# Building the matrices with C on their diagonals by DMA instead of by VectorE, in the state space scans of a four-layer network

## The chip, the core and the metric

The kernel runs on one core of a Trainium2 chip. Its engines are TensorE (PE, with its weight loads as PEld), VectorE (DVE), ScalarE (ACT), GpSimd (POOL) and SyncE (SP), which here issues nearly all transfers. Sixteen DMA engines move the data between DRAM and SBUF. The metric is the device time of one execution in microseconds (us). The time before the change is the median of 3 runs.

## The reference, cut to what matters

The reference applies four layers in turn, each as `x = x + layer(groupnorm(x))`, to an image batch of 4 x 96 x 56 x 56 in float32: softmax attention (layer 0), a selective scan in eight directions (layer 1), attention over the best eight of a local window (layer 2), and a scan in four directions with a bottleneck (layer 3). The change touches layer 1 alone. Its core, for each image, each of 8 directions, 192 channels and 16 states, over L = 3136 time steps:

```python
xs = cross_scan(xc)                      # rows, columns, diagonals, antidiagonals, and each backwards
x_dbl = einsum('bkdl,kcd->bkcl', xs, x_proj_weight)
dts, Bmat, Cmat = split(x_dbl, [R, R + N], axis=2)          # R = 6, N = 16
delta = softplus(einsum('bkrl,kdr->bkdl', dts, dt_projs_weight) + dt_projs_bias)
def step(hc, inp):
    u_t, d_t, B_t, C_t = inp
    hc = hc * exp(d_t[..., None] * A) + (d_t * u_t)[..., None] * B_t[:, :, None, :]
    return hc, einsum('bkdn,bkn->bkd', hc, C_t)
```

The last line is what the changed matrices serve: at each time step the 16 states of a channel are multiplied by that step's 16 values of C and added up.

## The kernel before

The layers follow one another. Layer 1 first projects, convolves and writes the four orders of the image to DRAM (`into_scan`), then runs `scans`, then gathers the eight directions and normalises. `scans` is the part that is changed, and all of it stands in one order written out by hand: within `in_order`, every engine executes its instructions exactly in the order in which the program issues them.

Two images lie together on the 128 partitions (64 channels each), the 192 channels are three blocks `j`, and the 3136 steps are seven chunks of 448. Two pairs, eight directions and seven chunks make 112 chunks. The 16 states are four groups `g` of four. A piece is (chunk, `j`, `g`), so a chunk has 12 pieces and the main loop (L712) turns 12 times for a chunk. In a turn:

- `inputs` (L614, POOL) makes `q` = delta times u times B for the piece two turns ahead, from `du` and the tile `bm` that holds B of the group, broadcast over partitions.
- `factor` (L622, ACT) makes `e` = exp(delta A), one state at a time, into three PSUM buffers, so up to three states ahead.
- `scan` (L634, DVE) runs four recurrences of 448 steps, in place in `q`; `carry` (L640, ACT) keeps the last state for the next chunk.
- `turned` (L650, PE) transposes the previous piece's `q`, `kept` (L659, ACT) copies it out of PSUM as `ht`, and `outputs` (L671, PE) multiplies it by `cd` and adds it to `y`. Time step t is m x 14 + c; after the transpose a partition is (state, m), with 4 states and 32 values of m. `cd` therefore holds, for every image half, group and c, a 128 x 32 matrix with four 32 x 32 diagonals, one for each state, and C on them. The matmul picks each step's own C and sums over the states.
- `gather` (L684, L685, DVE; L693, SP) copies a finished `y` and stores it after the third block.

Beside the twelve turns, the generator `prepare` makes what the next chunk needs. The main loop calls it once at the end of each of the turns 0 to 7, and `fetch` in turns 8 to 11:

- turn 0: load `u` (L551, SP); turn 2: project it (L557, PE), copy to `xd` (L561, ACT), store the rows of B and C to the DRAM tile `bc` (L564, SP, two DMAs)
- turn 3: load C from `bc` as `cv`, 128 partitions (state, m) of 112 values (L570, SP, two DMAs in pieces of 14 values)
- turn 5: project delta (L578, PE) and apply softplus (L580, ACT, with a change of the activation table before and after it), then VectorE multiplies `cv` by a repeated 32 x 32 identity (`same`) into `cd` (L585): 3584 values per partition, all but one in 32 of them zero
- turn 6: `du` = delta times u (L594, POOL)
- turns 8 to 11: `fetch` loads the four `bm` tiles (L604, SP, two DMAs each)

SP issues these in program order, and waits at an instruction until its operands have landed and its buffer is free. It runs ahead of the other engines where nothing holds it. There are six `bm` buffers, so SP can load the first two of the next chunk before the current chunk releases one. `out` is stored at turn 1, ahead of `bc`.

Of the kernel before, what the change touches and what calls it, by code (L numbers as in the profile page):

```python
# [9 lines left out]
F32 = mybir.dt.float32  # L10
AF = mybir.ActivationFunctionType
ALU = mybir.AluOpType
# [6 lines left out]
CH = 448  # L19
NCH = L // CH  # L20
# [25 lines left out]
def spread(ap, n):  # L46

    p, c = ap.shape
    return ap.unsqueeze(1).to_broadcast([p, n, c])
# [20 lines left out]
class Net:  # L70
# [435 lines left out]
    def scans(self, us, dram, ks):  # L506
# [3 lines left out]
        nc, tc = self.nc, self.tc  # L510
        ng = 4
        ngrp = NS // ng
        nk = len(ks)
        NT = 32
        NC = CH // NT
# [4 lines left out]
        with in_order(tc), ExitStack() as cx:  # L520
            wp = cx.enter_context(tc.tile_pool(name="sw", bufs=1))
            st1 = cx.enter_context(tc.tile_pool(name="sst", bufs=2))
            bp = cx.enter_context(tc.tile_pool(name="sbig", bufs=6))
# [3 lines left out]
            pst = cx.enter_context(tc.tile_pool(name="spt", bufs=2, space=PSUM))  # L527
            psy = cx.enter_context(tc.tile_pool(name="spy", bufs=1, space=PSUM))
            xpw, dtw, dtb, al = (self.load(wp, f"l1_{n}") for n in ("xpw", "dtw", "dtb", "alog"))
            same = self.load(wp, "k_same")  # L530
            na = wp.tile([128, nk, NB, NS], F32, name="na")
            nc.scalar.activation(na, al, AF.Exp)
            nc.vector.tensor_scalar(na, na, -1.0, None, ALU.mult)
# [1 line left out]
            def wide():  # L535
                return pst.tile([128, 2, 512], F32, name="t")

            chunks = []
            for pr in range(NPAIR):
                for k, (o, rev) in enumerate(ks):  # L540
                    for i in range(NCH):
                        chunks.append(dict(
                            pr=pr, k=k, src=us[pr][o], rev=rev, i=i, c=NCH - 1 - i if rev else i,
                        ))
            states = {}

            def prepare(s):

                k, c = s["k"], s["c"]
                u = p2.tile([128, NB, CH], F32, name="u", bufs=3)  # L550
                nc.sync.dma_start(u, s["src"][:, :, c * CH : (c + 1) * CH])  # L551
                s["u"] = u
                yield
                yield
                p = wide()[:, 0]
                for j in range(NB):
                    nc.tensor.matmul(  # L557
                        p[:, :CH], xpw[:, j, k, :], u[:, j, :], start=j == 0, stop=j == NB - 1
                    )
                xd = p2.tile([128, CH], F32, name="xd")  # L560
                nc.scalar.copy(xd, p[:, :CH])  # L561
                bc = dram.tile([2, 2 * NS, CH], F32, name="bc", tag="l1bc", bufs=4)
                for half in range(2):
                    nc.sync.dma_start(bc[half], xd[64 * half + R : 64 * half + R + 2 * NS, :])  # L564
                s["bc"] = bc
                yield
                cv = p2.tile([128, 2, ngrp, NC], F32, name="cv")
                for half in range(2):
                    c = bc[half, NS : 2 * NS]
                    nc.sync.dma_start(  # L570
                        cv[:, half], bass.AP(c.tensor, c.offset, [[NC, 128], [ng * CH, ngrp], [1, NC]])
                    )
                yield
                yield
                dl = s["dl"] = p2.tile([128, NB, CH], F32, name="dl")
                p = wide(), wide()
                for j in range(NB):
                    nc.tensor.matmul(p[j // 2][:, j % 2, :CH], dtw[:, k, j, :], xd, start=True, stop=True)  # L578
                for j in range(NB):
                    nc.scalar.activation(  # L580
                        dl[:, j, :], p[j // 2][:, j % 2, :CH], AF.Softplus, bias=dtb[:, j, k : k + 1]
                    )

                cd = s["cd"] = p2.tile([128, 2, ngrp, NC, NT], F32, name="cd")
                nc.vector.tensor_tensor(  # L585
                    cd.rearrange("p h g c m -> p (h g c) m"),
                    cv.rearrange("p h g c -> p (h g c)").unsqueeze(2).to_broadcast(
                        [128, 2 * ngrp * NC, NT]
                    ),
                    spread(same, 2 * ngrp * NC), ALU.mult,  # L590
                )
                yield
                du = s["du"] = p2.tile([128, NB, CH], F32, name="du")
                nc.gpsimd.tensor_tensor(du, dl, u, ALU.mult)  # L594
                s["bm"] = []
                yield
# [106 lines left out]
            for _ in prepare(chunks[0]):  # L703
                pass
# [7 lines left out]
            for at in range(len(pieces) + 1):  # L712
                p = pieces[at] if at < len(pieces) else None
# [3 lines left out]
                if p is not None and turn == 0:  # L717
                    s = p[0]
                    if s["i"] == 0:
                        states[s["pr"], s["k"]] = st1.tile([128, NB, NS], F32, name="state")  # L720
                    s["state"] = states[s["pr"], s["k"]]
                    nxt = chunks[at // per + 1] if at // per + 1 < len(chunks) else None
                    coming = prepare(nxt) if nxt is not None else iter(())
# [1077 lines left out]
```

## Time and profile before

| what | value |
|---|---|
| median of 3 runs | 16318.02 us (16299.98 to 16343.79) |
| profiled execution, time | 16344.06 us |
| profiled execution, span from first to last instruction | 16342.0 us |
| granted TensorE clock over the span | 0.916 |
| busy: PE / PEld | 13255.0 (81%) / 8983.5 us (55%) |
| busy: DVE / ACT / POOL | 13647.4 (84%) / 12214.4 (75%) / 7905.1 us (48%) |
| DMA | 821406 packets, 1152.54 MB |
| the product L585 | 112 times, 3.86 us each (median) |

Layer 1's scans lie between about 2430 and 8945 us of the span, so they fill slices 6 to 21 of the 40 slices of the page. Idle time of an engine that nothing later waits for costs nothing, so the questions to put to the profile are which engine sets the pace of a chunk, and what lies behind each transfer in SP's queue.

### The profile page before, as it was taken

Reading aid. Unit: us, or ns where it says so; the run is one execution under the profiler, and the core shown is the slowest. Engines: PE = TensorE matmul, PEld = TensorE weight load, DVE = VectorE, ACT = ScalarE, POOL = GpSimd, SP = SyncE. Lnnn points to the kernel's source line nnn. Section 1 sums busy time; section 2 is a strip of 40 time slices with the busy share of each in tenths; the row PEclk is TensorE's granted clock in tenths of the full one; section 3 lists DMA queues with packets and bytes.
Section 4 is the critical chain, followed back from the end, with each engine's and each line's share of the span. In section 5 each row is a group of like instructions: output and inputs, shape, how many; then the busy total and the mean of one; then the engine's idle time right before and its main releaser. Section 6 shows DMA issues by size and latency. Waiting matters only on the chain.

```text
span 16342.0 us, 501766 instructions
## 1 busy us (share of the span) xinstructions
PE 13255.0 (81%) x222032; PEld 8983.5 (55%) x222032; DVE 13647.4 (84%) x15363; ACT 12214.4 (75%) x15540; POOL 7905.1 (48%) x4079
## 2 busy tenths in 40 slices
PE   8999977777777777777776678878888888888876
PEld 4333326666666666666665555446666656566543
DVE  8666549999999999999998666768888888888866
ACT  0465448999999999999998245478888888888822
POOL 0000028888888888888887022123333333333300
PEclk7999889999999999999999579989999999999977
DMA  0000034333444443434444910222122222222122
GB/s 15 1 1 1 16 137 100 92 92 92 102 105 105 104 93 93 95 92 103 104 106 105 220 41 10 63 61 50 48 51 50 50 50 49 50 50 51 41 67 65
DMA packets 821406, 1152.54 MB, mean 71 GB/s; under 512 B 309360, under 2 KB 728720, under 8 KB 807456
## 3 DMA queue, kind: packets, MB, share of 16 engines
q1 hardware_dynamic: 759872, 1055.38, 26.6%
q10 hardware_dynamic: 53984, 45.77, 1.2%
q8 instruction: 1746, 28.61, 0.8%
q0 software_dynamic: 5376, 19.27, 0.4%
q14 instruction: 428, 3.51, 0.1%
HBM read 842.93 MB, written 277.18 MB: 69 GB/s over the span
## 4 chain that ended last, share of the span: by engine, by line
PE 34%; DVE 29%; ACT 20%; issue 12%; DMA 4%; POOL 1%; SPq 1%; DVEq 0%; ACTq 0%; POOLq 0%
DVE q L634 17%; PE q L1427 7%; ACT ht L659 5%; PE s L233 4%; ACT e L622 3%; PE d L413 3%; ACT phi L1375 3%; DVE w L1415 3%; PE z L1367 2%; PE acc L251 2%; PE m L196 2%; ACT w L1383 2%; PE y L671 2%; PE t L557 2%; PE t L650 2%
## 5 line engine op out<-in xcount | busy, mean ns | idle before, releaser
L614 POOL TENSOR_TENSOR q<-du,bm 128x1792 f32<-128x1792 f32 x1344 | 5348.3, 4026 | 3.1 <-DMA bm<-bc 3.1
L634 DVE TENSOR_TENSOR_SCAN q<-e,state,q 128x448 f32<-128x448 f32 x4608 | 4876.8, 1124 | 145.9 <-ACT e L622 141.9
L622 ACT ACTIVATE e<-dl,na 128x448 f32<-128x448 f32 x5376 | 3354.9, 640 | 173.7 <-DVE q L634 117.8
L671 PE MATMUL y<-ht,cd 128*32 128x64 f32 x75264 | 1838.4, 225 | 1470.2 <-ACT ht L659 1469.6
L650 PE MATMUL t<-ident,q 128*128 128x128 f32 x18816 | 2626.8, 293 | 93.7 <-issue 77.6
L1427 PE MATMUL q<-w,m 32*32 32x192 f32 x52224 | 2573.4, 348 | 125.8 <-DVE phi L1436 72.9
L650 PEld LDWEIGHTS t<-ident,q 128*128 128x128 f32 x18816 | 2391.2, 203 | 325.3 <-issue 203.3
L659 ACT COPY ht<-t 128x896 f32<-128x896 f32 x2688 | 2428.6, 904 | 101.2 <-PE t L650 70.6
L671 PEld LDWEIGHTS y<-ht,cd 128*32 128x32 f32 x75264 | 1400.3, 110 | 1948.2 <-ACT ht L659 1930.7
L1427 PEld LDWEIGHTS q<-w,m 32*32 32x32 f32 x52224 | 1873.5, 113 | 738.1 <-issue 182.2
L1436 DVE TENSOR_TENSOR phi<-q,phi 128x768 f32<-128x768 f32 x1632 | 1513.5, 953 | 523.9 <-PE q L1427 498.3
L1448 POOL TENSOR_TENSOR t<-t 128x384 f32<-128x384 f32 x408 | 407.2, 998 | 2977.2 <-DVE t L1447 2977.2
L241 ACT ACTIVATE e<-s 128x896 f32<-128x896 f32 (+1 forms) x1050 | 921.8, 915 | 913.7 <-PE m L196 516.2
L1367 PE MATMUL z<-ad,sm 32*32 32x256 f32 x39168 | 1277.1, 391 | 396.2 <-ACT phi L1375 382.6
L208 DVE TENSOR_REDUCE pm<-m 128x1 f32<-128x448 f32 (+1 forms) x1700 | 997.8, 618 | 688.6 <-PE m L196 641.4
L1375 ACT COPY phi<-z 128x1536 f32<-128x1536 f32 x816 | 1164.5, 1427 | 528.6 <-PE z L1367 528.4
L1415 DVE TENSOR_TENSOR w<-w,misc 128x3072 f32<-128x3072 f32 x408 | 1365.3, 3346 | 83.9 <-PE misc L1399 46.9
L1383 ACT ACTIVATE w<-phi,lntiny,w_k_rmask 128x3072 f32<-128x3072 f32 x408 | 1203.1, 2949 | 2.6
L196 PE MATMUL m<-ka,qa 32*128 32x448 f32 (+1 forms) x3400 | 1165.9, 628 | 9.0 <-DVE pm L208 7.5
L1391 ACT ACTIVATE phi<-phi,w_k_nmask 128x3072 f32<-128x3072 f32 x408 | 1165.6, 2857 | 2.4
L1367 PEld LDWEIGHTS z<-ad,sm 32*32 32x32 f32 x39168 | 709.1, 104 | 658.9 <-ACT phi L1375 465.2
L292 POOL DMA_DIRECT2D x<-xc x28 | 14.5, 517 | 2153.7 <-DVE xc L291 2152.8
(254 smaller groups left out, 18732.7 us busy)
## 6 DMA issues: line engine op xcount, KB each, us to landing
bm<-bc SPq DMA_DIRECT2D x896, 448.0 KB
cm<-cd SPq DMA_DIRECT2D x544, 186.0 KB
l1y<-out SPq DMA_DIRECT2D x672, 96.0 KB
l1y<-out SPq DMA_DIRECT2D x672, 72.0 KB
y<-l1y ACTq DMA_DIRECT2D x224, 168.0 KB
l3y<-y SPq DMA_DIRECT2D x1616, 23.2 KB
w<-l3cr SPq DMA_DIRECT2D x408, 48.0 KB
l3cr<-phi SPq DMA_DIRECT2D x408, 48.0 KB
```

Source lines behind the costliest of these rows:

```text
L614: nc.gpsimd.tensor_tensor(q, spread(s["du"][:, j, :], ng), s["bm"][g], ALU.mult)
L622: nc.scalar.activation(e[:, :CH], s["dl"][:, j, :], AF.Exp, scale=na[:, s["k"], j, n : n + 1])
L634: nc.vector.tensor_tensor_scan(a, e, a, first, ALU.mult, ALU.add)
L650: nc.tensor.transpose(flat(t)[:, 128 * c : 128 * c + 128], view(q, h * NC2 + c, [[NC, 128]]), self.ident,)
L659: nc.scalar.copy(t, flat(s["t", j, g, h])[:, : NC2 * 128])
L671: nc.tensor.matmul(s["y", j][r : r + 32, c // 4, 64 * half : 64 * half + 64], s["cd"][:, half, g, c, :], s["t", j, g, h][:, 128 * i + 64 * ...
L1367: nc.tensor.matmul(z[32 * b : 32 * b + 32, p, dh].rearrange("p n d -> p (n d)"), s["s"][ps_, dh, b, lo : lo + 32], st["ad"][ps_, dh, 8 * h ...
L1375: nc.scalar.copy(st["phi"][:, :, :, 8 * h : 8 * h + 8, :].rearrange("p a b n d -> p a b (n d)"), z.rearrange("p a b n d -> p a b (n d)"),)
L1383: nc.scalar.activation(w.rearrange("p a n d -> p (a n d)"), st["phi"].rearrange("p a b n d -> p (a b n d)"), AF.Sigmoid, bias=lntiny, scal ...
L1415: nc.vector.tensor_tensor(st["w"], st["w"], ut, ALU.mult)
L1427: nc.tensor.matmul(qp[bs, n, :DI], st["m"][bs, 4 * q + n, :], st["w"][bs, :, 4 * q + n, :], start=True, stop=True,)
L1436: nc.vector.tensor_tensor(ph, view(st[q], 0, [[256, 4], [32, 6], [1, 32]]), ph, ALU.mult)
```

## The change

The product by VectorE and its identity matrix go. In their place stand three DRAM arrays `cdz` of 128 x 112 x 32 values, which are filled with zeros once before the first chunk. For every chunk four DMAs write the values of `cv` one by one onto the diagonals of one of the three arrays (the addresses of a row's values are 128 bytes apart, and each row starts one value further), and one DMA loads the whole array, 1.8 MB, as `cd`. The off-diagonal zeros are never written again, so an array can be reused. The four DMAs stand at turn 4 and the load at turn 6, both on SP's queue, after `cv` and before the `bm` fetches.

```diff
             xpw, dtw, dtb, al = (self.load(wp, f"l1_{n}") for n in ("xpw", "dtw", "dtb", "alog"))
-            same = self.load(wp, "k_same")
+
+            ncol = 2 * ngrp * NC
+            cdz = [dram.tile([128, ncol, NT], F32, name=f"l1cdz{i}") for i in range(3)]
+            zero = bp.tile([128, ng, CH], F32, name="bm")
+            nc.gpsimd.memset(zero, 0.0)
+            for t in cdz:
+                for i in range(2):
+                    nc.sync.dma_start(
+                        t[:, i * ncol // 2 : (i + 1) * ncol // 2, :].rearrange("p c m -> p (c m)"),
+                        zero.rearrange("p n t -> p (n t)"),
+                    )
...
                         chunks.append(dict(
-                            pr=pr, k=k, src=us[pr][o], rev=rev, i=i, c=NCH - 1 - i if rev else i,
+                            at=len(chunks), pr=pr, k=k, src=us[pr][o], rev=rev, i=i, c=NCH - 1 - i if rev else i,
                         ))
...
                         cv[:, half], bass.AP(c.tensor, c.offset, [[NC, 128], [ng * CH, ngrp], [1, NC]])
                     )
                 yield
+                diag = cdz[s["at"] % 3]
+                for n in range(ng):
+                    nc.sync.dma_start(
+                        bass.AP(
+                            diag.tensor, diag.offset + n * NT * ncol * NT,
+                            [[ncol * NT + 1, NT], [NT, ncol]],
+                        ),
+                        cv[NT * n : NT * n + NT].rearrange("p h g c -> p (h g c)"),
+                    )
                 yield
                 dl = s["dl"] = p2.tile([128, NB, CH], F32, name="dl")
...
-
+                yield
                 cd = s["cd"] = p2.tile([128, 2, ngrp, NC, NT], F32, name="cd")
-                nc.vector.tensor_tensor(
-                    cd.rearrange("p h g c m -> p (h g c) m"),
-                    cv.rearrange("p h g c -> p (h g c)").unsqueeze(2).to_broadcast(
-                        [128, 2 * ngrp * NC, NT]
-                    ),
-                    spread(same, 2 * ngrp * NC), ALU.mult,
-                )
-                yield
+                nc.sync.dma_start(cd.rearrange("p h g c m -> p (h g c m)"), diag.rearrange("p c m -> p (c m)"))
                 du = s["du"] = p2.tile([128, NB, CH], F32, name="du")
                 nc.gpsimd.tensor_tensor(du, dl, u, ALU.mult)
```

## The prediction, as it was written before the changed kernel ran

> **What bounds the kernel now.** First the page's busy rows over the 40 slices, then the busy time of a steady stretch of the scans (columns: PE, PEld, DVE, ACT, POOL busy, clock, DMA share, GB/s), its groups by form and its waits (us, times, longest), then one chunk in order of time.
>
> ```profile
> DVE  8666549999999999999998666768888888888866
> ACT  0465448999999999999998245478888888888822
> 3000.00:8300.00 5300.00, 4034.26 (x78088) 3299.93 (x78078) 5132.05 (x5041) 4896.04 (x8096) 4646.11 (x1192) 0.98 0.42 98
> L585 DVE TENSOR_TENSOR cd<-cv,w_k_same 128x3584 f32<-128x3584 f32 x92 | 355.0, 3858 | 0.0
> ACT xd L561 <- PE t L557: 184.8, 91, 2.1
> ACT e L622 <- DVE q L634: 85.5, 326, 0.4
> ```
>
> In the scans both VectorE and ScalarE are full. The stretch of 5300 us holds 92 chunks, so a chunk takes 57.6 us (57.8 over all of them): VectorE 55.8 busy, ScalarE 53.2, POOL 50.5, DMA 42%. The product takes 3.86 us of VectorE. But of ScalarE's 4.4 idle us a chunk, 2.0 wait for PE's projection and only 0.93 for VectorE. One chunk shows why (VectorE, ScalarE, POOL and SP, merged, start and duration in us):
>
> ```profile
> 6568.63 5.28 DVE L634 TENSOR_TENSOR_SCAN q<-e,state,q 128x448 f32<-128x448 f32 x5
> 6585.40 0.78 SPq L564 DMA_DIRECT2D bc<-xd  x2
> 6586.94 0.93 SPq L570 DMA_DIRECT2D cv<-bc  x2
> 6587.97 20.88 SPq L604 DMA_DIRECT2D bm<-bc  x8
> 6596.78 3.86 DVE L585 TENSOR_TENSOR cd<-cv,w_k_same 128x3584 f32<-128x3584 f32 x1
> 6597.65 1.28 ACT L580 ACT_TABLE_LOAD   x1
> 6598.94 1.68 ACT L580 ACTIVATE dl<-t,w_l_dtb 128x448 f32<-128x448 f32 x3
> 6600.64 1.28 ACT L622 ACT_TABLE_LOAD   x1
> 6601.94 0.64 ACT L622 ACTIVATE e<-dl,na 128x448 f32<-128x448 f32 x1
> 6603.72 47.75 POOL L614 TENSOR_TENSOR q<-du,bm 128x1792 f32<-128x1792 f32 x12
> ```
>
> The reader is to see two things. The product stands exactly where ScalarE is away from `e` for 4.3 us, from 6597.65 to 6601.94. And SP issues `bm` at 6587.97, right behind `cv`, though POOL needs the first group only for the fourth of its twelve operations, at 6603.72 + 3 x 3.98 = 6615.7. That one ends at 6619.7, and its scan is due at 6568.63 + 57.8 = 6626.4. So `bm` is early by a lot.
>
> **The change, part by part.** *The product goes.* Without it the scans of turn 6 start at 6596.8 on the three states in hand, and end at 6600.0. The fourth `e` is there only at 6602.6, so its scan ends at 6603.7. The next turn follows ScalarE (`e` at 6603.95, 6605.3, 6605.9), and turn 8 starts at 6608.55, where before it started at 6600.56 + 8 x 1.047 = 6608.94. The gain is 0.4 us a chunk, not 3.86: ScalarE's table changes are late next. Over 111 chunks that is -44 us. The first chunk's product lay beside its `bm` loads.
>
> *Five DMAs more on SP, ahead of `bm`.* The load of `cd` waits on SP until all four diagonal DMAs have landed, and behind it stand the eight `bm` DMAs, the next `u` and the stores of `out`. The `bm` DMAs are what POOL waits for. The chain from chunk to chunk, when it binds:
>
> - first scan to `bc`: 6585.40 - 6568.63 = 16.8
> - `bc` to `cv` 1.5; `cv` to its landing 2.4 (its packets are seen until 6589.1)
> - the diagonals, T
> - issue of the `cd` load 0.5; 1.835 MB at the rate of the weight load, another plain load of long rows, 426 GB/s: 4.3 (at the rate of `bm`, which rereads rows, 223 GB/s: 8.2; the kind of row decides for 426)
> - first `bm` group, 0.918 MB at 223 GB/s: 4.1; landing 0.8, what `bc` needs after its issue
> - POOL's operation 4.0
>
> The sum is 34.4 + T. As long as it is under 57.4 the transfers are hidden, behind the 6.7 us by which POOL is early and the time in which `bm` lay ready. T = 23.0 is the point from which the chain decides.
>
> *T.* A chunk writes 128 x 112 = 14336 values, each a packet of its own, 896 for each of 16 engines. The trace has no 4-byte store to DRAM from a tile. The rows near it, by window (packets, MB, share of 16 engines): the loads of `cv` with packets of 56 bytes over 1.25 us; the shortest stores to DRAM, 372 bytes in layer 3 (`cd<-x`), over 0.6 us; and for the rates above, weights and `bm`, over 6 us each.
>
> ```profile
> q1 hardware_dynamic: 1043, 0.06, 58.6%
> ...
> q1 hardware_dynamic: 80, 0.02, 22.4%
> ...
> q1 hardware_dynamic: 224, 2.56, 100.4%
> ...
> q1 hardware_dynamic: 221, 1.34, 99.9%
> ```
>
> The loads cost 0.586 x 16 x 1250 / 1043 = 11.2 ns of engine time a packet, and 17.6 ns of elapsed time with 64 to an engine in about 1.13 us. The stores cost 0.224 x 16 x 600 / 80 = 26.9 ns. So T is 10.0 + 1.2 = 11.2 us (17 by elapsed time) by the one, 24.1 + 1.2 = 25.3 us by the other, where 1.2 is the time from the last issue to the landing that `bc` shows. I take the store: it is the row of the same kind, a short piece from SBUF into DRAM, though its longer piece may make it too dear.
>
> [...]
>
> *Once.* Zeros for three arrays, 5.5 MB at 426 GB/s: 12.9 us ahead of the first `u` on the same queue. The first chunk's `bm` comes 1.4 + T + 0.5 + 4.3 later, with nothing to hide it: 44 us in all at T = 25.3, 30 at 11.2. POOL's memset lies beside the weight loads.
>
> *At no cost:* the three arrays and two `cd` buffers, reused after chunks; `dl` and `du` in the turns where they stood; DMA share (24.3 busy us a chunk + 24.1 + 4.3 = 53 under 59.7, so the order on the queue and not the sum of bytes decides). If the cover of early `bm` were gone, each us of T would cost 111 us.
>
> *Sum.* 34.4 + 25.3 = 59.7 against 57.8: +1.9 a chunk, +211; with +44 it is +255 us. The profiled execution took 16344 us (span 16342.0), so 16599. It stood 26 us above the median of the runs, 16318, so the forecast is 16573.
>
> **The rivals.** *Hidden.* If a value costs what a short load costs (11 to 18 ns), or anything under 24.3 ns an engine, T stays under 23 and nothing waits. Then the 44 us gained by VectorE meet 30 to 36 us at the start: 16344 - 11 = 16333, or 16307 against the median, no change that can be told (about 0.3%, 49 us, is what a measurement of this kernel can tell). For it: the loads' row, and that packets from 56 bytes up grow dearer mainly by their bytes. Against it: they are loads. Here the change may also be faster by more: if ScalarE's 0.93 us of waits for VectorE went too, -103 + 33 = -70, 16248. The whole 3.86 us is excluded, since ScalarE's 53.2 busy us and its 2.0 for the projection remain: at most -2.6 a chunk, -255 with the start.
>
> [...]
>
> **How the numbers follow.** Price of a short store, T from about 23.4 to 41 us: 0.42, forecast 16573. Hidden: 0.46, of which 0.30 within 0.3%, 0.14 faster, 0.02 slower by the start alone. Two passes or near it: 0.12. So faster 0.14, same 0.30, slower 0.42 + 0.02 + 0.12 = 0.56. The range begins at 16230, a little below the 16248 of the hidden case with ScalarE's waits gone, and ends at 18300, where T is 40.8 us and a value costs 44 ns; about 0.06 lies under it and 0.14 over it. The likeliest case alone spans 16370 to 18300.
>
> **What would show it.** Right: L585 gone; SP waiting at the `cd` load for the diagonals, some 25 us after the first of them; POOL waiting about 2 us a chunk for `bm`; VectorE's idle time growing from 1.8 to about 7.8 us a chunk (59.7 - 51.9), part of it behind ScalarE after the tables; a chunk of 59.7 us. The hidden case would show POOL without a wait for DMA, and chunks of 57.4. The forecast is wrong at its root if the diagonals land within 23 us (too high) or take over 41 (too low), and in its first part if a chunk with `bm` in time comes down by over 1 us.

## The result, and the profile after

The changed kernel takes 16963.98 us (median of 4 runs, 16947.79 to 17004.64) where the kernel before takes 16315.32 us beside it: 1.0395 times as long, 95% interval 1.0380 to 1.0411. The forecast was 16573. The direction was right, and the chain from chunk to chunk does bind as the forecast said; but the move is +649 us where +255 was forecast. The profiled execution took 16979.03 us.

The page's busy rows of the changed kernel, slices as before:

```profile
DVE  8656458888888888888888776568888888888866
ACT  0556438888888888888888525558888888888822
```

The steady stretch (PE, PEld, DVE, ACT, POOL busy, clock, DMA share, GB/s):

```profile
3000.00:8300.00 5300.00, 3832.57 (x71608) 3140.98 (x71605) 4429.40 (x4542) 4476.26 (x7422) 4265.80 (x1094) 0.93 0.94 119
```

And the waits in the same stretch (us in all, times, longest):

```profile
POOL q L626 <- DMA bm<-bc: 631.1, 101, 14.5
...
ACT e L634 <- DVE q L646: 469.2, 205, 8.6
DVE q L646 <- POOL q L626: 422.4, 94, 8.3
...
ACT xd L571 <- PE t L567: 170.8, 84, 2.1
```

In slices 6 to 21 the nines of VectorE and ScalarE have become eights. The stretch now holds 84 chunks instead of 92. Three rows of waits that were absent or small tell the order: POOL waits for the DMA of `bm`, VectorE for POOL's `q`, ScalarE for VectorE. The wait of `xd` for PE's projection, 2.0 us a chunk, is as it was. One chunk, VectorE, SP and POOL merged in order of time (start, duration, and in brackets the idle time before and what ended it):

```profile
6587.70 5.32 DVE L646 TENSOR_TENSOR_SCAN q<-e,state,q 128x448 f32<-128x448 f32 x5 [3.31 <-POOL q L626]
6604.95 0.79 SPq L574 DMA_DIRECT2D bc<-xd  x2
6606.50 0.94 SPq L580 DMA_DIRECT2D cv<-bc  x2
6609.15 14.09 SPq L586 DMA_DIRECT2D l1cdz<-cv  x4
6633.80 0.34 SPq L604 DMA_DIRECT2D cd<-l1cdz  x1
6634.19 8.68 SPq L616 DMA_DIRECT2D bm<-bc  x8
6646.74 11.89 POOL L626 TENSOR_TENSOR q<-du,bm 128x1792 f32<-128x1792 f32 x3 [11.45 <-DMA bm<-bc]
6650.76 5.32 DVE L646 TENSOR_TENSOR_SCAN q<-e,state,q 128x448 f32<-128x448 f32 x5 [4.04 <-POOL q L626]
```

Read the starts as a chain: 17.25 to `bc`, 1.55 to `cv`, 2.65 to the first scatter, 24.65 until SP can issue the load of `cd`, 12.94 until POOL has its first `bm`, 4.02 until VectorE has `q`. The sum is 63.06 us from first scan to first scan. The SP row at L586 shows something else: the issue of the four scatters alone keeps SP for 14 us.

Means over all 111 chunk changes, from the starts of the same lines, beside the forecast's terms:

| term | forecast | changed kernel |
|---|---|---|
| first scan to `bc` | 16.8 | 17.1 |
| `bc` to `cv`, `cv` to the scatter | 1.5 + 2.4 | 1.7 + 2.9 |
| T, the scatter until the load of `cd` is issued | 25.3 | 24.1 |
| `cd` issue to POOL's first operation on the new `bm` | 0.5 + 4.3 + 4.1 + 0.8 = 9.7 | 13.2 |
| POOL's operation | 4.0 | 4.0 |
| a chunk | 59.7 | 63.0 |

To place the whole difference, the span is cut at three marks: the load of the weights `w_l_xpw` (L85), the first scan, and the last scan of layer 1.

| part of the span | before | changed | difference |
|---|---|---|---|
| ahead of the weights | 2428.4 | 2408.6 | -19.8 |
| weights to first scan | 32.0 | 77.1 | +45.1 |
| first scans of the first to the last chunk | 6417.1 | 6995.6 | +578.5 |
| the last chunk's own scans | 50.9 | 51.0 | +0.1 |
| layers 2 and 3, and what lies between | 7413.5 | 7444.9 | +31.4 |
| span | 16342.0 | 16977.3 | +635.3 |

The first and the last part are untouched by the change. Over all kernels below, the part ahead of the weights is between 2373 and 2428 us and the last between 7414 and 7457, in no order that follows an edit. So the experiments are read by their ratios, and where less than one per cent matters by the third row, called the scans' time, which is free of that spread.

### The profile page after: what moved, and what is told of

Same layout as the page of the kernel before. It is cut to its first block, busy times and chain, and to the rows that moved or that the text cites. A ratio compares the mean times of both kernels' runs of the same rounds, so it can differ in the third digit from the quotient of the medians.

```text
span 16977.3 us, 502116 instructions
## 1 busy us (share of the span) xinstructions
PE 13454.4 (79%) x222032; PEld 9140.1 (54%) x222032; DVE 13275.9 (78%) x15251; ACT 12196.7 (72%) x15540; POOL 7904.9 (47%) x4080
## 3 DMA queue, kind: packets, MB, share of 16 engines
q8 instruction: 1746, 28.61, 0.8%
## 5 line engine op out<-in xcount | busy, mean ns | idle before, releaser
L683 PE MATMUL y<-ht,cd 128*32 128x64 f32 x75264 | 1935.1, 232 | 1860.3 <-ACT ht L671 1833.8
L662 PE MATMUL t<-ident,q 128*128 128x128 f32 x18816 | 2716.5, 300 | 135.1 <-issue 69.0
L683 PEld LDWEIGHTS y<-ht,cd 128*32 128x32 f32 x75264 | 1478.3, 114 | 2357.0 <-ACT ht L671 2298.5
L662 PEld LDWEIGHTS t<-ident,q 128*128 128x128 f32 x18816 | 2467.3, 204 | 371.7 <-issue 189.6
```

The lines of the kernel that those rows point to most:

```text
L662: nc.tensor.transpose(flat(t)[:, 128 * c : 128 * c + 128], view(q, h * NC2 + c, [[NC, 128]]), self.ident,)
L683: nc.tensor.matmul(s["y", j][r : r + 32, c // 4, 64 * half : 64 * half + 64], s["cd"][:, half, g, c, :], s["t", j, g, h][:, 128 * i + 64 * ...
```

## The experiments

Two questions stood after this: which terms of the chain are needed for the loss, and what the change costs where the chain does not bind. The theory was that SP's order (scatter, load of `cd`, then `bm`) makes POOL late. The first rival was that the single values slow the other transfers or engines wherever they stand.

**No product, no transfers.** The kernel before without the product; `cd` is a constant tile.

```diff
-                cd = s["cd"] = p2.tile([128, 2, ngrp, NC, NT], F32, name="cd")
-                nc.vector.tensor_tensor(cd..., cv..., spread(same, ...), ALU.mult)
+                s["cd"] = fixed
```

> Neither the product nor any of the diagonal transfers: the matrices are a constant tile set once, so y is not the reference's. It shows what VectorE's product alone was worth. Theory 1 (ScalarE's table changes stand where the product stood, 0.4 us a chunk gained): 16315 - 45 = 16270 us, ratio 0.997. Rival (VectorE was the bound, so each chunk gains the product's 3.86 us): 16315 - 430 = 15885 us, ratio 0.974.

Measured: 16300.73 us against 16317.35, ratio 0.9982 (0.9971 to 0.9994); the scans take 6391.0 us instead of 6417.1, 0.24 us a chunk less. The wait that took the product's place, in the stretch from 3000 to 8300:

```profile
DVE q L628 <- ACT e L616: 450.1, 620, 2.8
```

Before, VectorE waited for `e` for 151.7 us there. The 298 us more over 92 chunks are 3.2 us of the product's 3.86 a chunk: VectorE has the time and ScalarE does not. So if `cd` came from elsewhere at no cost at all, the gain would be 0.18% (0.06 to 0.29).

**Scatter only.** The kernel before with the four scatters of each chunk added; VectorE still makes `cd`, and nothing reads the arrays.

```diff
                 yield
+                diag = cdz[s["at"] % 3]
+                for n in range(ng):
+                    nc.sync.dma_start(bass.AP(diag.tensor, ...), cv[NT * n : NT * n + NT]...)
                 yield
```

> The kernel before with its product by VectorE, plus the four diagonal DMAs at turn 4, whose arrays nobody loads. SP waits for nothing, but the B tiles stand behind 14336 single values in the rings. Theory 1 (only the chain from chunk to chunk counts): 17.1 + 1.6 + 2.8 + 23 + 7.1 + 4.0 = 55.6 us a chunk, under the 57.8 of before, so 16315 to 16340 us. Rival (the DMA engines, 94% busy in the changed kernel, slow whatever runs beside them): over 16500 us.

Measured: 16482.19 us, ratio 1.0100 (1.0075 to 1.0124). This fits neither expectation. The chain does not bind (from POOL's first operation on the new `bm` to the scan that needs it are 11.2 us, of which the operation is 4.0), and yet a chunk is 59.06 us, 1.25 more. The row that has grown is PE's, and it has no releaser: "issue" is time in which the engine waited for nothing that the profile shows. First the kernel before, then this one, both over 3000 to 8300:

```profile
PE t L650 <- issue: 64.3, 92, 0.7
```

```profile
PE t L661 <- issue: 108.7, 118, 3.2
PE y L682 <- issue: 94.8, 93, 2.8
```

Before, `y` has no such row. The 139 us more are 1.55 us for each of the 90 chunks in the stretch: enough for the whole loss. That it reaches ScalarE, one of the two full engines, is seen in ScalarE's waits for PE's transposes, before and here:

```profile
ACT ht L659 <- PE t L650: 59.3, 87, 1.2
```

```profile
ACT ht L670 <- PE t L661: 191.9, 187, 3.8
```

Before, none of these waits is over 1.3 us; here 45 are, 99.6 us in all, and half of them follow a stop of PE by under 1.9 us. The granted TensorE clock is lower too, 0.97 over the stretch where before has 0.98, but a transpose takes 295 ns instead of 294, so the clock explains little of it.

**B first.** The changed kernel with two of the four `bm` groups ahead of the scatter, and the load of `cd` (now in `place`) behind the fourth. All of the computation is there.

```diff
                 yield
+                s["bm"] = []
+                fetch(s)
+                fetch(s)
                 diag = cdz[s["at"] % 3]
...
-                    fetch(nxt)
+                    if turn < 2 * ngrp + 2:
+                        fetch(nxt)
+                    elif turn == 2 * ngrp + 2:
+                        place(nxt)
```

> All of the changed kernel, in another order on SP: the first two B tiles of the next chunk are fetched right behind cv, ahead of the diagonals, and the load of cd comes after the last two B tiles, at turn 10. Theory 1: the diagonals leave the chain, a chunk takes about 57.4 us and the time is 16290 to 16330 us. Rival (share of the DMA engines, not the order, costs the time): it stays above 16600 us.

Measured: 16408.15 us, ratio 1.0053 (1.0033 to 1.0072), above the range expected. The same bytes, the same scatter and the same load, in another order, take back 556 of the 649 us: POOL's wait for `bm` is

```profile
POOL q L633 <- DMA bm<-bc: 5.3, 8, 1.4
```

instead of 631.1, and the start falls from 77.1 to 45.3 us. So the order on SP's queue is shown as the cause of most of the loss. (Not all of the 556 us is its share, since this run's chip takes the scatter some 4 us faster, as the repeat below shows. On the chip of the repeat, the paced kernel, which has B first too, takes back 391 of 661 us in spite of a wait of its own.) What is left is PE's "issue" again: its rows are 79.7 and 48.5 us here, 0.70 us a chunk above the kernel without transfers, and the scans are 0.78 a chunk longer than there.

**Small load.** The changed kernel with 32 values a partition loaded instead of 3584, and a constant `cd`.

```diff
-                nc.sync.dma_start(cd.rearrange(...), diag.rearrange("p c m -> p (c m)"))
+                few = p2.tile([128, NT], F32, name="few")
+                nc.sync.dma_start(few, diag[:, 0, :])
+                s["cd"] = fixed
```

> The changed kernel with its diagonals, its wait and its place on SP, but the load behind the wait brings 32 values per partition instead of 3584, and the matmuls use a constant tile, so y is not the reference's. In the changed kernel 13.2 us pass from the issue of the load to POOL's first product of the next chunk. Theory 1 (6.1 us of it is the load of cd): 63.0 - 6.1 = 56.9, so the chunk falls to the 57.4 of VectorE and ScalarE, about 16330 us with the zero fill. Rival (the load takes 4.3 us as estimated, the B tile the rest): 58.7 us a chunk, about 16435 us.

Measured: 16455.25 us, ratio 1.0083 (1.0057 to 1.0109). From the issue of the small load to POOL's operation are 7.6 us where the full load has 13.2. So the full load is worth 5.6 us of the chain, and one `bm` group takes some 7.2 us from its issue to its use (7.6 less the 0.4 of the small load's issue). T is 19.9 us here and not 24.1 (the repeat below returns to it); the chain sums to 53.5 us and does not bind any more. The time is near the rival's 16435, but by luck: the rival had the chain bind at 58.7 us, whereas the chunk of 58.6 us here goes with PE's "issue", 104.4 and 64.0 us.

**Pieces of 64 bytes.** The same number of packets, but each carries 16 values instead of one, 64 bytes that start at a multiple of 128. The arrays then do not hold C on their diagonals.

```diff
-                            [[ncol * NT + 1, NT], [NT, ncol]],
+                            [[ncol * NT, NT], [NT, ncol], [1, 16]],
```

> The changed kernel, but each of the 14336 pieces of a chunk is 64 bytes long and starts at a multiple of 128 bytes, instead of 4 bytes; the arrays then do not hold C on diagonals, so y is not the reference's. [...] Rival (the number of packets decides, whatever their length): T stays at 20 to 24 us or grows, and the time stays at 16800 us or more.

Measured: 16495.86 us, ratio 1.0108 (1.0092 to 1.0124). T falls to 13.4 us, since the 14336 packets go out in 10.9 us instead of 20.3 (from the start of the first to the end of the last). Sixteen times the bytes take half the time, so the number of packets alone does not decide, and the rival is excluded. The chain does not bind, yet the kernel is 1.1% slower, with PE's "issue" at 118.8 and 95.5 us: again the second effect alone.

**Load only.** The changed kernel without the scatters; the load of `cd` stays, and loads zeros.

```diff
-                for n in range(ng):
-                    nc.sync.dma_start(bass.AP(diag.tensor, ...), cv[...])
```

> The changed kernel without the four diagonal DMAs: the arrays stay zero, so y is not the reference's; the 1.8 MB load of cd stays in its place. Theory 1 (PE's late instructions come from the 4-byte packets): PE's waits put down to issue go back to those of the kernel before, a chunk takes 57.6 us as without transfers, and the time is 16300 to 16320 us. Rival (any load on the DMA engines makes PE late): 16350 us or more. The load itself: its packets should run at 426 GB/s from the start if the slow first 2 us in the changed kernel come from DRAM still taking in the diagonals.

Measured: 16357.68 us against 16309.71, ratio 1.0029 (1.0017 to 1.0041). The scans take 6401.0 us, 10 more than without any transfer, and the start 51.4, 19 more than before. The load is hidden in the steady chunk, and PE's "issue" rows are as in the kernel without transfers, 64.4 and 3.1 us. So the sign of the theory is there, though the time is where the rival put it. Scans and start together account for about 3 us against the kernel before; the rest of the 48 us is not explained. (The two profiled executions differ by 15 us, and 12 of them lie in the parts that the change does not touch.)

**The changed kernel again**, on the chip of the last two.

> The changed kernel again, beside the others on their chip, to compare its stages with theirs: T was 24.1 us in its first profile, and 19.9 us in the run that loads 32 values per partition. If the difference belongs to the chip, T comes out near 20 here and the time near 16500 to 16600 us; if it belongs to the full load, T stays near 24 and the time near 16960 us.

Measured: 16970.95 us, ratio 1.0402 (1.0381 to 1.0423); T is 24.0 us and a chunk 63.1. This was to decide whether the longer T, 24 where the small load has 20, belongs to the chip or to the full load. But it ran on chip 6 and the small load on chip 8, so it alone cannot. The packets of all the profiles can. Between the 4500th and the 7000th value of a burst, 0.82 to 0.84 values a ns leave in the three kernels that ran on chip 8 (scatter only, B first, small load), and 0.60 to 0.65 in all others: this one, the first profile of the changed kernel (its chip is not on record), and those on chips 6 and 13 below. On either side there are kernels with the load of `cd` and without it. So the rate goes with the chip and not with the load. The changed kernel has no run that is known to be on chip 8; with T at 20 its chain would take 58.9 us, an estimate from its other terms.

**Paced.** B first, and POOL copies quarters of `cv`, which has one buffer here, at four turns, so that the scatters should go out one by one.

```diff
+                cw = p2.tile([128, 2 * ngrp * NC], F32, name="cw", bufs=1)
+                def write(n):
+                    nc.gpsimd.tensor_copy(cw[rows], cv[rows]...)
+                    nc.sync.dma_start(bass.AP(diag.tensor, ...), cw[rows])
+                write(0)
                 yield
+                write(1)
```

> All of the changed kernel in the order of the run with the first two B tiles ahead of the diagonals, and the four diagonal DMAs are paced: POOL copies a quarter of cv at the ends of turns 4, 5, 6 and 7, and each DMA takes its quarter, so that 3584 values go out at a time, some 4 us apart. Theory 1 (a long backlog of 4-byte packets delays PE's instruction transfers, a burst under about 4000 is taken in fast): PE's waits for issue go back towards those of before, and the time is 16300 to 16330 us. Rival (the values delay them whatever the pace): as with the B tiles first, about 16410 us.

Measured: 16579.68 us, ratio 1.0159 (1.0142 to 1.0176). The pacing did not come about: SP still issued the four within 20.1 us (mean; B first has 17.9), and POOL now stands in a wait of its own, `cw` for `cv`, 244.8 us in 85 times. It says nothing of smaller bursts.

**Half the values, and two bursts.** With the scatter-only kernel as base, first two of the four scatters alone, then all four with two of them (in `rest`, which only the second kernel has) behind the fourth fetch of B.

```diff
-                for n in range(ng):
+                for n in range(ng // 2):
...
+                    if turn == per - 1:
+                        rest(nxt)
```

> The kernel before with only the first two of the four transfers that scatter C into the DRAM array in each chunk, and the array is not read (the output is still computed from VectorE's product). All four together cost 1.0100, that is 163 us, though nothing waits for them. Theory of the backlog: instruction transfers arrive late because they stand behind queued single values, so both the number of those hit and the time each waits grow with the length of the burst; half a burst costs a quarter, +41 us, 1.0025, with PE's waits for issue near 75 + 25 us over 3000 to 8300. Rival, a price for each value wherever it stands: half of it, +82 us, 1.0050, with PE's waits for issue near 86 + 47 us.

> The kernel before with all four scatter transfers in each chunk, array not read, but the last two stand behind the fourth fetch of B instead of beside the first two, so that the same 14336 values go out as two bursts of half the length some 20 us apart. Theory of the backlog: two quarters, +82 us, 1.0050. Rival, a price for each value: as with all four together, +163 us, 1.0100, with PE's waits for issue again near 109 + 95 us.

Measured: half, 16432.10 us, ratio 1.0069 (1.0053 to 1.0085), with "issue" at 86.6 and 91.3 us; two bursts, 16499.91 us, 1.0103 (1.0086 to 1.0119), with 104.4 and 113.1. Half the values cost more than half, and cutting the burst brought nothing. The theory in the form given, cost as the square of the burst, falls. But the rival fits the half badly too, at 1.0069 where it wanted 1.0050; a part of that is the chip, on which half the values take 9.0 us where all took 16.7 with the scatter only.

**B first, two bursts.** The two edits together, with all of the computation.

> The changed kernel with the first two groups of B ahead of the first two scatter transfers, the other two behind the third fetch of B, and the load of cd behind the fourth. All of the computation is there. With B first and one burst the time was 1.0053 (+87 us). Theory of the backlog: the part that is PE's late instructions (about 0.5 of the 0.55 us a chunk) halves, so 1.0020 to 1.0035, +35 to +57 us. Rival, a price for each value: 1.0050. If the second burst, now beside later fetches of B, makes POOL wait for B or PE for cd, more than 1.0060, with rows of waits for bm or cd to show it.

Measured: 16493.46 us, ratio 1.0102 (1.0086 to 1.0119). The third case of the expectation came: beside the second burst the later fetches of B and the load of `cd` come late.

```profile
POOL q L643 <- DMA bm<-bc: 109.9, 44, 5.6
...
PE y L700 <- DMA cd<-l1cdz: 80.2, 44, 4.3
```

**Long rows in the place of the scatter.** The kernel without product and transfers, with four stores of 1.835 MB in rows of 14336 bytes where the scatter was.

```diff
                 yield
+                for t in cdz:
+                    nc.sync.dma_start(
+                        t.rearrange("p c m -> p (c m)"), fixed.rearrange("p h g c m -> p (h g c m)")
+                    )
                 yield
```

> The kernel without the product, the scatter and the load of cd (cd is a constant tile, so the values of C don't enter the output; that kernel took 0.9982), with four stores of 1.835 MB in rows of 14336 bytes put at the place of the scatter, into four DRAM arrays that nothing reads. By the rate of other long rows (426 GB/s) they keep the DMA engines busy for some 17 us, as long as the scatter does, and push the loads of B back by as much. Theory that the single values themselves make PE's instructions late: PE's waits for issue stay near 64 + 3 us over 3000 to 8300, 16300 to 16340 us, 0.998 to 1.001. Rival, that any backlog of that length ahead of B does it, by B's loads standing later and together: waits near 109 + 95, +1.4 us a chunk, 16420 to 16470, 1.006 to 1.010.

Measured: 16542.36 us against 16342.05, ratio 1.0119 (1.0097 to 1.0141). The theory of the single values falls, and the rival stands, at more than it asked for. Against the kernel that it is built on, the scans are 217 us longer, 1.96 us a chunk, and PE's waits are

```profile
PE t L650 <- issue: 125.3, 124, 3.4
...
PE y L671 <- issue: 129.7, 112, 2.9
```

With no small packet added, PE loses more than with any scatter, and ScalarE's wait for the transposes is 253.9 us instead of 53.0. One place shows what "issue" is (weight loads of PE, some 33 us after the first of the four stores of that chunk):

```profile
6537.62 0.50 PEld L671 LDWEIGHTS y<-ht,fixed 128*32 128x32 f32 x24 [0.86 <-ACT ht L659]
6540.59 0.25 PEld L671 LDWEIGHTS y<-ht,fixed 128*32 128x32 f32 x4 [2.47 <-issue]
```

A half of `outputs` is 28 weight loads for one and the same `ht`. After 24 of them PE stops for 2.47 us, with its operands there and nothing to wait for, and then does the last 4. What it lacks is instructions. These come by DMA too, in transfers of 16 KB on the page's instruction queue q8 (1746 of them, 28.61 MB, before and changed alike), about 6.7 a chunk in every kernel. (PE's 222032 matmuls and as many weight loads over the 1746 transfers make 254 a transfer.) One of them starts in the half microsecond from 6537.5:

```profile
q8 instruction: 1, 0.02, 16.6%
```

It starts at 6537.62, ends at 6538.95, and PE goes on 1.64 us later. This holds throughout. In the stretch from 3000 to 8300 there are 101 stops for "issue" of over 0.5 us ahead of a weight load of `outputs`, and all 101 end 1.2 to 1.9 us after a transfer of q8 has ended; so do all 82 of the scatter-only kernel, where of moments taken at random 8% would. So it is shown that PE stands until its next block of instructions is in, and that q8 is PE's. Counting their starts over the stretch from 3000 to 8300, by the time since the first added transfer of the chunk (for the two kernels without one, since `cv`, some 1 us sooner or 3):

| instruction transfers in the stretch | 0 to 18 us | 18 to 30 us | 30 to 42 us | a chunk, first 30 us |
|---|---|---|---|---|
| before | 177 | 132 | 149 | 3.4 |
| no product, no transfers | 179 | 132 | 149 | 3.4 |
| scatter only | 163 | 81 | 183 | 2.7 |
| half the values | 92 | 153 | 189 | 2.7 |
| long rows | 139 | 92 | 191 | 2.6 |

While the queue holds the added transfers and the 3.67 MB of `bm` behind them, 0.7 to 0.8 of PE's blocks a chunk are not brought in time; they follow when the backlog ends. The share of the engines by queue in 30 us from such a moment, first the kernel with long rows (from 6507.7 us), then the kernel before (from `cv`, 6587.9 us):

```profile
q1 hardware_dynamic: 2068, 9.96, 99.7%
```

```profile
q1 hardware_dynamic: 2096, 4.42, 64.7%
```

Before, a third of the engines' time is free, because SP waits for POOL between the `bm` groups:

```profile
SPq L604 <- POOL q L614: 1471.4, 219, 13.7
```

A long transfer put ahead of `bm` takes this time away, since the `bm` groups then find their buffers free and go out in one piece; a short one does not. The same wait of SP is 1406 us in the load-only kernel, whose PE rows have not grown, 513 with half the values, 261 with the scatter only and 302 with long rows. That the free time is what hides the instruction transfers is the reading that fits these rows; it was not tried apart from them.

## Why the prediction was right or wrong

*The product.* Forecast: worth 0.4 us a chunk, not 3.86, since ScalarE is late next. Right in kind: 0.24, and VectorE's wait for `e` took its place. The rival with all ScalarE waits gone (16248) is excluded by that run.

*T.* Forecast 25.3, measured 24.1. The store row (26.9 ns of engine time) was nearer than the load row (11.2): 14336 packets leave in 20.3 us, 22.7 ns for each of an engine's 896. But the agreement is in part luck. The row was a mixture: of its 80 packets 64 carry 372 bytes and took 31.1 ns each, and 16 carry 4 bytes and took 9.8. No one price of a short store stands behind it, since pieces of 64 bytes went out at 12.2 ns for each of an engine's 896. And T depends on the chip, as the repeat showed: with T at 20 the chain would take 58.9 us where 59.7 was forecast, near it by two errors that cancel. The 0.12 for two passes was for a value at twice the store's 26.9 ns, an estimate of the author. No run shows such a price: the values left at 22.7 ns, and T was 24.1 us. Why the single values take 20.3 us, where 64-byte pieces at the same 128-byte steps took 10.9, is not shown.

*The step that failed* is the term behind T: "issue of the `cd` load 0.5", its 4.3 us, the first `bm` group at 4.1 and the landing at 0.8, together 9.7. It measured 13.2, and 3.5 us times 111 chunks is 388 us, the whole of the miss (the other terms of the chain give +1.0 and -1.2 us a chunk). Both transfers were priced as bytes over the rate of a long stream, and both take longer from issue to use. The load of `cd` begins on empty engines. Its first two windows of the chunk shown, 2.5 and 3.5 us from its issue (packets, MB, share of 16 engines):

```profile
q1 hardware_dynamic: 27, 0.39, 63.6%
...
q1 hardware_dynamic: 105, 1.42, 95.2%
```

That is 155 GB/s, then 406. By the packets, the first starts 1.0 us after the issue, the first twenty take 1.1 us each and the later ones 0.56; over all chunks the 120th of the load's 128 ends 6.3 us after the issue and the last 8.1. The packets take the same time where no scatter went before (load only: 1.1, then 0.56), so the scatter is not to blame. And a `bm` group of 0.918 MB needs 7.1 us from issue to use, not 4.9. That row stood in the trace of before, at the first chunk, where only the end of the load of `cv` is ahead of it:

```profile
2448.71 4.98 SPq L604 DMA_DIRECT2D bm<-bc  x8
...
2455.86 20.33 POOL L614 TENSOR_TENSOR q<-du,bm 128x1792 f32<-128x1792 f32 x5 [3.05 <-DMA bm<-bc]
```

From 2448.71 to 2455.86 are 7.15 us: 1.3 to the first packet, 4.6 for 128 packets, the size of the group, and 1.3 more until POOL begins. The forecast had nothing, 4.1 and 0.8. Had it taken the latency of this row rather than bytes over rate, it would have had 0.5 + 4.3 + 7.1 = 11.9, a chunk of 61.9 and +500 us with the start. The point from which the chain decides also moves, from T = 23.0 to 57.4 - 38.9 = 18.5, with 38.9 what the chain measures without T. So the hidden case, which had 0.46, needed a T under 18.5.

*Start.* Forecast +44, measured +45.1 between the weights and the first scan.

*At no cost.* "DMA share ... so the order on the queue and not the sum of bytes decides" held for the changed kernel, and B first shows it. It failed for what lies beside: with a fuller queue PE's instructions come late (PE's "issue" is 2.9 us a chunk with long rows, 0.7 before). In the changed kernel itself this is covered by the chain (its "issue" rows are 54.7 us and 20.1 over 84 chunks, 0.9 a chunk where before has 0.7); it appears once the order is mended, and is most of what keeps B first at 1.0053. The forecast had no such term. No version here that makes `cd` in full beats the kernel before.

The sum, against the profiled executions: 255 forecast, +367 for a chunk of 63.0 instead of 59.7, +1 for the start, +12 in the layers that the change does not touch, is 635.

## What to carry to other kernels

A term of a chain is the time from issue to use, taken from a row where the queue was empty; bytes over the rate of a long stream came out short of it here, by 3.5 us on every chunk. A wait on a queue costs what stands behind it, so put transfers that nothing needs soon, and whose issue waits, behind those that the next engine waits for: the same transfers in another order cost 0.5% instead of 4.0% (on one and the same chip 1.6%, with a wait of POOL added). And when PE stops for "issue" in the middle of equal instructions, look at what fills the queues: here all 183 such stops of two kernels ended just after a transfer of instructions, and with the DMA engines 99.7% busy over 30 us of a chunk instead of 64.7%, PE's "issue" was 2.9 us a chunk instead of 0.7. That the idle time of the DMA engines makes this difference is a reading, as said above.

## What the runs showed of the hardware

- Single values of 4 bytes from SBUF to DRAM, 128 bytes apart: about 4000 have left 3.65 us after the issue, then the rate falls from some 1.4 to 0.65 packets a ns (0.82 to 0.84 in the three kernels on chip 8, which showed 1.6 at first). SP's issue takes 14.1 us for the four transfers, where four stores of long rows took 3.2. In the chunk shown, the first 4 us and the next 18 us from the first issue:

```profile
DMA packets 4388, 0.02 MB, mean 4 GB/s; under 512 B 4388, under 2 KB 4388, under 8 KB 4388
```

```profile
DMA packets 9909, 0.07 MB, mean 4 GB/s; under 512 B 9907, under 2 KB 9907, under 8 KB 9907
```

- PE goes on 1.2 to 1.9 us after the block of instructions that it stood for has come in (all of 183 stops in two kernels; in the changed kernel 14 of 17, the other three 2.1 to 3.0 us). Instruction transfers that start 4 to 9 us after the first scatter take 2.6 us with half the values (median of 48), where before, after `cv`, they take 1.3; beside long rows they take 0.9 and still come late. So with long rows the delay lies before the transfer starts. What holds it there is not shown: the trace has no time of request.
- In the kernel before, the DMA engines are 64.7% busy in the 30 us from `cv`, and PE's "issue" comes to 0.7 us a chunk (64.3 us over 92 chunks). With long rows they are 99.7% busy in such a stretch, and it is 2.9 us (255.0 us over 89 chunks).
- Open: why single values leave faster on one chip than on two others, with the same scatter; and how PE's delay depends on the length of the backlog, since half the values cost 0.69 of all and two bursts as much as one.
